# Layer 1 of a four-layer model: its preparation in a written order, the second half's decays among the chunks, the experts six steps later

## The chip, the cores and the metric

The kernel runs on one core of a Trainium2 chip. A core has five engines with queues of their own: TensorE (PE; its weight loads are shown as PEld), VectorE (DVE), ScalarE (ACT), GpSimd (POOL) and SyncE (SP), which here only issues transfers. The metric is device time in microseconds (us) from launch to end; lower is better. Each engine works through its queue in order, and an instruction that waits holds up everything behind it on its engine.

## The reference, cut to what matters

The model has four layers, each an attention-like part plus a feed-forward part on the same normed input. The kernel has B = 2 sequences of S = 1024 tokens with D = 128. The change is in layer 1 alone: gated slot attention (4 heads, K = V = 32, M = 64 slots) beside a mixture of eight experts with the top two picked.

```python
xn = _layernorm(x, axis=-1)
x = x + _L1_attn_ref(xn, ...) + _L1_ffn_ref(xn, ...)

# attention
q = _swish((x @ Wq).reshape(b, t, H, K))
k = _swish((x @ Wk).reshape(b, t, H, K))
v = (x @ Wv).reshape(b, t, H, V)
f = jax.nn.log_sigmoid((x @ Wf).reshape(b, t, H, M)) / GATE_LOGIT_NORMALIZER   # 8
s = 1.0 - jnp.exp(f)
def step(carry, inp):
    hk, hv = carry
    q_t, k_t, v_t, s_t, g_t = inp
    ge = jnp.exp(g_t)
    hk = hk * ge[:, :, None, :] + k_t[..., :, None] * s_t[..., None, :]
    logits = jnp.einsum('bhk,bhkm->bhm', q_t * scale, hk)
    p = jax.nn.softmax(logits, axis=-1)
    hv = hv * ge[..., :, None] + s_t[..., :, None] * v_t[..., None, :]
    return ((hk, hv), jnp.einsum('bhm,bhmv->bhv', p, hv))
o = o * rsqrt(mean(o * o) + NORM_EPS) * g_norm_w
return o.reshape(b, t, H * V) @ Wo

# experts
probs = jax.nn.softmax(x @ gate_w.T, axis=-1)
top2_w, top2_idx = jax.lax.top_k(probs, 2)
h = jax.nn.relu(jnp.einsum('th,ehf->tef', x, W1) + b1)
y = jnp.einsum('teh,ehf->tef', h, W2) + b2
out = jnp.einsum('te,tef->tf', comb, y)
```

## The kernel before

Activations lie transposed in SBUF: `xT` and the normed `xnT` are 128 features by 2048 tokens in f32, batch 0 in the first 1024 columns. `layer1` (L1612) norms, then runs two generators in turn: `l1_gsa`, the attention, and `l1_experts`. Each `yield` is a mark; `in_turn` (L1076) goes from mark to mark of the attention, numbers them n, and after each mark for which `when(n)` holds lets the experts go one piece further.

`l1_gsa` first prepares (up to L1393), with three PSUM buffers of two banks. For each batch: queries and keys (`l_pq`, L1344, Silu on ACT), then keys and values by rows (`l_pk`, L1353: `l_kt` by ACT, `l_vt` by DVE). Then four gate units, each one half of the slots (a) of one batch over all 1024 tokens: `l_pz` is the product with Wf; ACT does Abs, Exp, Ln (L1366 to L1368), DVE the subtraction that makes the log gate (L1369), ACT exponentials of plus and minus an eighth of it (`l_up`, `l_g`), and DVE the decays: 1 - g into `l_sf`, one scan for `l_ef` and one for its inverse `l_r` (L1381, a running product that starts anew every 128 tokens), and three products into `l_sf`. ACT loads a table whenever it changes among Silu, Exp and Ln. `stat` and `c.bad` collect whether the decays stayed in range. In this part a planner set the order of the instructions on each engine.

Then come 16 chunks j (n = j // 2 is the 128 tokens, b = j % 2 the batch), in an order written out by hand (`manual_schedule`, L1523), with four marks to a chunk. For chunk j: `l_pa`, masked into `l_at` (`pairs`); `l_sf` and `l_ef` turned by PE into `l_pr`, copied to `l_se` by ACT (`turned`); the logits `l_lg`, DVE's `l_p` and `l_m`, four Exp on ACT (`logits`); DVE's shares (`shares`); the end decay `l_pd`, `l_dk`; the states `l_pu`, `l_hk`, `l_hv`; and one chunk later the turned shares `l_pp`, `l_pt`, the weights `l_pw`, `l_wt` and the outputs `l_po`, copied into `l_oT`. `l_po` and `l_pu` share one PSUM buffer. After the loop the outputs are normed (`l_ms`) and multiplied with Wo.

The experts' pieces (`moe_sparse`, L746): the routing (`l1_route`: weights `r_w_t`, logits `r_lg`, softmax, both top picks); the rows turned (`m_pr`, `m_rows`) and each token's slot (`places`: `m_used`, `m_rank`, ..., `m_to`, `m_back`); 32 scatters of 128 rows each on POOL's queue into the slots in DRAM (L780), in four pieces; loads of the first two experts by SP; then for each of eight experts four pieces: rows in (`m_pt`, `m_xeT`), first product (`m_ph`, `m_h`), second product (`m_py`, `m_yT`), rows out (`m_pb`, `m_ye`, stored by SP), with the load for the expert after next; then eight pieces that gather two tiles of rows each (four gathers on POOL's queue, L840, one piece ahead), weigh them (`m_rows`) and turn them back (`m_back`) into xT. With `lead=2` two pieces come before the attention's first mark; four follow in the preparation, the experts begin at mark 14 (chunk 2), and from 48 on every second mark has a piece.

Of the kernel before, what the change touches and what calls it, by code (L numbers as in the profile page):

```python
# [10 lines left out]
F32 = mybir.dt.float32  # L11
BF16 = mybir.dt.bfloat16
I32 = mybir.dt.int32
AF = mybir.ActivationFunctionType
# [4 lines left out]
P = 128  # L19
# [1264 lines left out]
def l1_gsa(c, w, xnT, oT):  # L1284
# [7 lines left out]
    with ExitStack() as es:  # L1292
# [34 lines left out]
        stat = wp.tile([P, 4 * NTB], F32, tag="stat", name="stat")  # L1327

        q, k, kt, vt = ([None] * B for _ in range(4))
        ef, sf = [], []  # L1330

        qds = []
        for n in range(4):
            qds.append(wp.tile([P, L1_H, P], F32, tag=f"qd{n}", name=f"l1_qd{n}"))
            nc.gpsimd.memset(qds[n], 0.0)
        with tc.tile_pool(name="g_ps0", bufs=3, space=PSUM) as ps:
            for b in range(B):
                xb = xnT[:, b * S : (b + 1) * S]
                q[b] = sb.tile([P, S], F32, tag=f"q{b}", name=f"l1_q{b}")
                k[b] = sb.tile([P, S], F32, tag=f"k{b}", name=f"l1_k{b}")  # L1340
                for n, dst in enumerate((q[b], k[b])):
                    pq = ps.tile([P, S], F32, tag="mm", name=f"l1_pq{b}_{n}")
                    mm_wide(c, pq, wqk[:, n, :], xb)
                    nc.scalar.activation(dst, pq, AF.Silu)  # L1344
                kt[b] = sb.tile([P, NTB, D], F32, tag=f"kt{b}", name=f"l1_kt{b}")
                vt[b] = sb.tile([P, NTB, D], F32, tag=f"vt{b}", name=f"l1_vt{b}")
                for g in range(2):
                    gs = slice(4 * g, 4 * g + 4)
                    pk = ps.tile([P, 4, 2, D], F32, tag="mm", name=f"l1_pk{b}_{g}")
                    for n in range(4):  # L1350
                        t = 4 * g + n
                        mm(c, pk[:, n], xb[:, t * P : (t + 1) * P], wkv.rearrange("p a d -> p (a d)"))
                    nc.scalar.activation(kt[b][:, gs, :], pk[:, :, 0, :], AF.Silu)  # L1353
                    nc.vector.tensor_copy(vt[b][:, gs, :], pk[:, :, 1, :])
                yield
            for b in range(B):
                xb = xnT[:, b * S : (b + 1) * S]
                ef.append(sb.tile([P, 2, S], F32, tag=f"ef{b}", name=f"l1_ef{b}"))
                sf.append(sb.tile([P, 2, S], F32, tag=f"sf{b}", name=f"l1_sf{b}"))
                for a in range(2):  # L1360
                    pz = ps.tile([P, S], F32, tag="mm", name=f"l1_pz{b}_{a}")
                    mm_wide(c, pz, wf[:, a * P : (a + 1) * P], xb)
                    at = 2 * b + a

                    g = wk.tile([P, S], F32, tag="g", name=f"l1_g{b}_{a}")
                    nc.scalar.activation(g, pz, AF.Abs)  # L1366
                    nc.scalar.activation(g, g, AF.Exp, scale=-1.0)
                    nc.scalar.activation(g, g, AF.Ln, bias=1.0)  # L1368
                    nc.vector.scalar_tensor_tensor(g, pz, 0.0, g, ALU.min, ALU.subtract)  # L1369
                    up = wk.tile([P, S], F32, tag="up", name=f"l1_up{b}_{a}", bufs=1)  # L1370
                    nc.scalar.activation(up, g, AF.Exp, scale=-0.125)
                    nc.scalar.activation(g, g, AF.Exp, scale=0.125)
                    s = sf[b][:, a, :]
                    nc.vector.tensor_scalar(s, g, -1.0, 1.0, ALU.mult, ALU.add)

                    e = ef[b][:, a, :]
                    r = wk.tile([P, S], F32, tag="r", name=f"l1_r{b}_{a}", bufs=1)
                    for x, y in ((g, e), (up, r)):
                        nc.vector.tensor_copy(first[:, 0:S:P], x[:, 0:S:P])
                        nc.vector.memset(x[:, 0:S:P], 0.0)  # L1380
                        nc.vector.tensor_tensor_scan(y, x, first, 0.0, ALU.mult, ALU.add)  # L1381
                    nc.vector.tensor_scalar(
                        stat[:, at * NTB : (at + 1) * NTB], e[:, P - 1 : S : P], 1e-14, None, ALU.is_ge
                    )

                    tt(c, g, e, r, ALU.mult)
                    nc.vector.scalar_tensor_tensor(g, g, 2.0, r, ALU.subtract, ALU.mult)
                    nc.vector.scalar_tensor_tensor(s, g, -1.0, s, ALU.mult, ALU.mult)
                    yield

            ok = wp.tile([P, 1], F32, tag="ok", name="l1_okp")
            nc.vector.tensor_reduce(ok, stat, AX.X, ALU.min)
            nc.vector.tensor_scalar(c.bad[:, 1:2], ok, 0.5, None, ALU.is_lt)  # L1393

        with tc.tile_pool(name="g_ps", bufs=1, space=PSUM) as ps:
            NJ = B * NTB
# [13 lines left out]
            def pairs(j):  # L1410
# [4 lines left out]
                ats[j] = wk.tile([P, L1_H, P], F32, tag="at", name=f"l1_at{tag}")  # L1415
                tt(c, ats[j], pa, bcast_mid(upto, L1_H), ALU.mult)

            def turned(j):

                n, b, ts, tag = where(j)  # L1420
                pr = ps.tile([P, 2, 2 * P], F32, tag="pr", name=f"l1_pr{tag}")
                for a in range(2):
                    nc.tensor.transpose(pr[:, 0, a * P : (a + 1) * P], sf[b][:, a, ts], c.ident)
                for a in range(2):
                    nc.tensor.transpose(pr[:, 1, a * P : (a + 1) * P], ef[b][:, a, ts], c.ident)
                ses[j] = wk.tile([P, 2, 2 * P], F32, tag="se", name=f"l1_se{tag}", bufs=3)
                nc.scalar.copy(ses[j], pr)

# [37 lines left out]
            def weights(j):  # L1466
                n, b, ts, tag = where(j)

                pw = ps.tile([P, 2, 2, 2 * P], F32, tag="pw", name=f"l1_pw{tag}")
                for h in range(L1_H):  # L1470
                    a, r = divmod(h, 2)
                    rows = slice(HF * r, HF * r + HF)
                    mm(c, pw[:, r, a, 0:P], sf[b][rows, a, ts], pts[j][rows, a, :])
                wts[j] = wk.tile([P, 2, 2, P], F32, tag="wt", name=f"l1_wt{tag}")
                tt(c, wts[j].rearrange("p r a t -> p (r a) t"), pw.rearrange("p r a t -> p (r a) t")[:, :, 0:P],
                   bcast_mid(upto, 4), ALU.mult)
# [20 lines left out]
            def states(j, dk):  # L1497

                n, b, ts, tag = where(j)
                ss = ses[j][:, 0, :]  # L1500
                pu = ps.tile([P, HM + P], F32, tag="pu", name=f"l1_pu{tag}")
                mm(c, pu[:, 0:HM], kt[b][:, n, :], ss)
                for a in range(2):
                    mm(c, pu[:, HM + a * HF : HM + (a + 1) * HF], ss[:, a * P : (a + 1) * P],
                       vt[b][:, n, a * HF : (a + 1) * HF])
                nk = wk.tile([P, HM], F32, tag=f"hk{b}", name=f"l1_hk{tag}")
                nv = wk.tile([P, 2, HF], F32, tag=f"hv{b}", name=f"l1_hv{tag}")
                uk, uv = pu[:, 0:HM], pu[:, HM:].rearrange("p (a v) -> p a v", v=HF)
                if n:
                    tt(c, nk, uk, hk[b], ALU.add)  # L1510
                    uk = nk
                    tt(c, nv, uv, hv[b], ALU.add)
                    uv = nv
                tt(c, nk, uk, dk.rearrange("p h m -> p (h m)"), ALU.mult)
                end = (n + 1) * P - 1
                for a in range(2):
                    nc.vector.scalar_tensor_tensor(
                        nv[:, a, :], uv[:, a, :], ef[b][:, a, end : end + 1], vmask.rearrange("p a v -> p (a v)"),
                        ALU.mult, ALU.mult,
                    )  # L1520
                hk[b], hv[b] = nk, nv

            with tc.manual_schedule():  # L1523
# [2 lines left out]
                pairs(0)  # L1526
                turned(0)
                old = {}
                for j in range(NJ + 1):
                    if j:  # L1530
                        turn_shares(j - 1)
                    if j < NJ:
                        old[j] = hv[j % B]
                        logits(j)
                        yield
                    if j:
                        weights(j - 1)
                    if j < NJ:
                        if j + 1 < NJ:
                            pairs(j + 1)  # L1540
                        yield
                        if j + 1 < NJ:
                            turned(j + 1)
                        shares(j)
                        if j < NJ - B:
                            dk = end_decay(j)
                        yield
                    if j:
                        outputs(j - 1, old.pop(j - 1))
                    if j < NJ:  # L1550
                        yield
                        if j < NJ - B:
                            states(j, dk)
# [58 lines left out]
def layer1(c, w, xT, xnT, general=False):  # L1612
    nc, tc = c.nc, c.tc
    layernorm_all(c, xT, xnT, 1e-5, "n1")
    with tc.tile_pool(name="l1", bufs=1) as sb:
# [3 lines left out]
        with tc.tile_pool(name="e1", bufs=1) as s2, tc.tile_pool(name="e1_ps", bufs=2, space=PSUM) as ps:  # L1619
# [4 lines left out]
            else:  # L1624

                in_turn(
                    l1_gsa(c, w, xnT, oT), moe, lead=2,
                    when=lambda n: n < 4 or 14 <= n < 47 or (n > 47 and n % 2 == 0),
                )
        if general:  # L1630
            l1_gsa_scan(c, w, xnT, oT)
# [640 lines left out]
```

## Time and profile before

| | us |
|---|---|
| median of 3 runs | 2033.06 (2029.17 to 2038.33) |
| the profiled execution | 2022.65 |
| its span, first to last instruction | 2020.9 |
| its mean granted TensorE clock | 0.882 |

Busy time by layer, from the profile's stretches (the borders are read from the timeline; a stretch has norm and experts in it):

| stretch, us | what | PE | DVE | ACT | POOL | clock |
|---|---|---|---|---|---|---|
| 0 to 1160 | layer 0 | 1008.5 | 692.7 | 808.0 | 73.7 | 0.92 |
| 1160 to 1425 | layer 1 | 186.2 | 145.6 | 150.1 | 82.2 | 0.77 |
| 1425 to 2021 | layers 2 and 3 | 439.9 | 425.9 | 307.8 | 257.7 | 0.85 |

In layer 1, by line:

| line, engine | what | count | mean ns |
|---|---|---|---|
| L1381 DVE | scans over 128x1024 | 8 | 2290 |
| L1369 DVE | log gate, 128x1024 | 4 | 1216 |
| L63, L1387, L1388 DVE | the three products, 128x1024 each | 12 | 1219 |
| L1366 to L1368, L1371, L1372 ACT | Abs, Exp, Ln, Exp, Exp, 128x1024 | 20 | 1050 |
| ACT | table loads, 1179 to 1265 | 12 | 1283 |
| L780 POOL | scatters | 32 | 1459 |

How it is read: times count from the span's first instruction. A busy PE is not PE at its peak, since matmuls are pipelined and their ends modelled; a clock of 1.00 is full speed, 0.50 half. An f32 product shows as two records for each of its instructions. In the names of the profile, buffer numbers are left out: `l_pz` is every gate product.

### The profile page before, as it was taken

How to read it: one execution, taken by the hardware profiler on the slowest of the kernel's cores; microseconds unless marked ns; L12 is line 12 of the kernel's file. 1: busy time of each engine (PE TensorE's matmuls, PEld its weight loads, DVE VectorE, ACT ScalarE, POOL GpSimd, SP SyncE). 2: the span in 40 equal slices, each digit the busy share in tenths (PEclk: the TensorE clock that was granted, in tenths of full speed). 3: DMA queues.
4: the chain of work that ended last, by engine and by line, in shares of the span. 5: the costliest groups of instructions: out<-in, count | busy, mean ns of one | idle time of the engine just before them, and what ended most of it. 6: DMA issues, size and time to landing. Idle time of an engine off the chain costs nothing. (4 is left out here: it accounts for less than half of the span.)

```text
span 2020.9 us, 18408 instructions
## 1 busy us (share of the span) xinstructions
PE 1634.6 (81%) x5978; PEld 730.2 (36%) x5978; DVE 1264.2 (63%) x2130; ACT 1265.9 (63%) x2116; POOL 413.6 (20%) x413
## 2 busy tenths in 40 slices
PE   4699999999688789988888772987785999566784
PEld 2232322222234334433333340654332444223563
DVE  4788866881365446446556338554457998785673
ACT  3378756786477787887877665654556778223451
POOL 2000000000000200000300017033056666761110
PEclk7799989999788899999999885986787999778897
DMA  4521110100100210100100001110014443100000
GB/s 107 161 63 32 25 26 2 25 1 2 48 6 12 62 31 26 31 21 16 38 5 0 8 12 35 58 43 23 9 37 152 136 161 102 42 15 18 6 6 12
DMA packets 76817, 81.66 MB, mean 40 GB/s; under 512 B 12759, under 2 KB 57590, under 8 KB 75560
## 3 DMA queue, kind: packets, MB, share of 16 engines
q1 hardware_dynamic: 67224, 62.68, 10.5%
q0 software_dynamic: 7888, 16.93, 3.4%
q8 instruction: 49, 0.80, 0.2%
q10 hardware_dynamic: 1600, 0.79, 0.2%
q14 instruction: 56, 0.46, 0.1%
HBM read 55.18 MB, written 24.44 MB: 39 GB/s over the span
## 5 line engine op out<-in xcount | busy, mean ns | idle before, releaser
L487 DVE TENSOR_REDUCE maxes<-sc 128x1 f32<-128x1024 f32 x256 | 303.6, 1219 | 79.1 <-PE sc L51 78.3
L602 ACT ACTIVATE ex<-st 128x512 f32<-128x512 f32 x512 | 277.1, 599 | 102.9 <-PE st L51 97.5
L51 PE MATMUL st<-qst,kst 75*128 75x512 bf16 x512 | 178.7, 391 | 8.4 <-DMA qst<-mt 5.6
L51 PE MATMUL sc<-kst,qst 72*128 72x512 bf16 x512 | 161.1, 399 | 28.0 <-DMA kst<-scr 14.1
L1786 POOL TENSOR_TENSOR su<-dx,bb 128x512 f32<-128x512 f32 x128 | 162.3, 1273 | 83.1 <-DVE sh L1797 76.2
L780 POOL DMA_INDIRECT m_x<-m_rows,m_to x80 | 98.6, 1232 | 335.6 <-DVE m_back L742 188.8
L840 POOL DMA_INDIRECT m_yg<-m_y,m_back x80 | 79.8, 998 | 422.9 <-DVE a_y L1045 311.2
L51 PE MATMUL py<-spr,ident 128*128 128x512 f32 x256 | 146.9, 658 | 0.0
L1792 ACT ACTIVATE da<-dt,am 128x512 f32<-128x512 f32 x128 | 87.6, 690 | 83.4 <-DVE sh L1797 79.4
L51 PE MATMUL av<-ex,va 128*9 128x512 f32 x1024 | 139.2, 613 | 0.0
L51 PE MATMUL a_ph<-a_x,wf 128*128 128x512 f32 x256 | 122.6, 614 | 12.7 <-DVE a_x L1046 9.3
L51 PE MATMUL a_pf<-a_h,wf 128*128 128x512 f32 x256 | 114.1, 599 | 0.0
L51 PE MATMUL pc<-cst,sel 80*128 80x512 bf16 x128 | 52.8, 413 | 74.9 <-DVE spr L63 71.0
L51 PEld LDWEIGHTS <-kst 75*128 75x128 bf16 x512 | 49.1, 98 | 168.9 <-issue 126.3
L1007 ACT ACTIVATE a_h<-a_ph,cols 128x512 f32<-128x512 f32 x128 | 84.9, 687 | 33.4 <-PE a_ph L51 33.2
L51 PEld LDWEIGHTS py<-spr,ident 128*128 128x128 f32 x256 | 53.3, 209 | 126.4 <-issue 99.9
L51 PE MATMUL a_pQ<-a_y,wqkvo 128*128 128x512 f32 x56 | 48.0, 1007 | 53.7 <-DVE a_y L1046 53.7
L63 DVE TENSOR_TENSOR spr<-sh,pc 128x512 f32<-128x512 f32 x128 | 85.3, 667 | 8.1 <-PE pc L51 7.9
L63 DVE TENSOR_TENSOR a_r<-a_r,a_x 128x512 f32<-128x512 f32 x32 | 22.0, 690 | 99.1 <-ACT a_r L1018 99.1
L1797 DVE TENSOR_TENSOR_SCAN sh<-da,su 128x512 f32<-128x512 f32 x64 | 77.9, 1217 | 7.5 <-POOL su L1786 4.0
L51 PEld LDWEIGHTS <-qst 72*128 72x128 bf16 x512 | 51.5, 101 | 85.7 <-issue 45.4
L1797 DVE TENSOR_TENSOR_SCAN sh<-da,carry,su 128x512 f32<-128x512 f32 x64 | 81.7, 1276 | 0.2 <-ACT carry L1839 0.2
(541 smaller groups left out, 3224.0 us busy)
## 6 DMA issues: line engine op xcount, KB each, us to landing
bb<-bd SPq DMA_DIRECT2D x64, 256.0 KB
m_w<-in_L_ffn_w_dram SPq DMA_DIRECT2D x44, 128.0 KB
m_xe<-m_x SPq DMA_DIRECT2D x22, 256.0 KB
m_y<-m_ye SPq DMA_DIRECT2D x22, 256.0 KB
qst<-scr POOLq DMA_DIRECT2D x24, 192.0 KB, 9.1
kst<-scr SPq DMA_DIRECT2D x24, 192.0 KB
wf<-in_L_attn_Wf_dram SPq DMA_DIRECT2D x16, 256.0 KB
m_x<-zero SPq DMA_DIRECT2D x1, 3584.0 KB
```

The lines of the kernel that those rows point to most:

```text
L51: c.nc.tensor.matmul(out, lhsT, rhs, start=start, stop=stop)
L63: c.nc.vector.tensor_tensor(out, a, b, op)
L487: nc.vector.tensor_reduce(mx[:, t % HT, i : i + 1], sc, AX.X, ALU.max)
L602: nc.scalar.activation(ex, st, AF.Exp)
L780: nc.gpsimd.indirect_dma_start(views[K * t + k][:, :], bass.IndirectOffsetOnAxis(ap=to[:, k, t : t + 1], axis=0), rows[:, t, :], None)
L840: nc.gpsimd.indirect_dma_start(g, None, ys[:, :], bass.IndirectOffsetOnAxis(ap=back[:, k, t : t + 1], axis=0))
L1007: nc.scalar.activation(half(b, f"h{f}", o, "h", f"h{l}_{b}_{f}_{o}", bufs=8), ph, AF.Gelu_apprx_tanh, bias=c.cols["bf1"][:, 4 * l + f : 4 ...
L1786: nc.gpsimd.tensor_tensor(us[k], dx[b, a][:, o * CH : (o + 1) * CH], bb[2 * b + o, s], ALU.mult)
L1792: nc.scalar.activation(das[k], dt[b, a][:, o * CH : (o + 1) * CH], AF.Exp, scale=am[:, a, s : s + 1])
L1797: nc.vector.tensor_tensor_scan(hs[k], das[k], us[k], carry[b, a][:, s : s + 1] if o else 0.0, ALU.mult, ALU.add)
```

## The change

The order of the preparation is written out, under `manual_schedule`, and its marks change. A gate unit is now one half of the tokens (u) of one batch with both halves of the slots, so `ef` and `sf` have four tiles of 128x2x512 in place of two of 128x2x1024; the scans run over 512 columns; Abs and Exp write into `ef` itself, and `r` lies in `up`. The first halves of both batches come first (products, logs, exponentials), then a mark with the routing behind it, then the second halves' products and logs and the first unit's decays, then five marks (slots, scatters). Queries, keys and values follow, with the second unit's decays around them. The second halves' exponentials and decays are done one piece at a time among the chunks (`more()`, one at each mark; two units, eight pieces each: chunks 0 to 3). `lead=2` goes; the experts' pieces come at marks 0 to 5, 20 to 58 and then at every even one, where the preparation has six marks as before: experts begin at the last mark of chunk 3 in place of chunk 2's.

```diff
+        UNITS = [(b, u) for u in range(2) for b in range(B)]
...
+        def gate_products(b, u, ps):
+            pz = pzs[b, u] = ps.tile([P, 2, CH], F32, tag="mm", name=f"l1_pz{b}_{u}")
+            for a in range(2):
+                mm(c, pz[:, a, :], wf[:, a * P : (a + 1) * P], xnT[:, b * S + u * CH : b * S + (u + 1) * CH])
+
+            f = ef[b, u]
+            nc.scalar.activation(f, pz, AF.Abs)
+            nc.scalar.activation(f, f, AF.Exp, scale=-1.0)
+
+        def gate_logs(b, u):
+            nc.scalar.activation(ef[b, u], ef[b, u], AF.Ln, bias=1.0)
+
+        def log_gates(b, u):
+            nc.vector.scalar_tensor_tensor(ef[b, u], pzs[b, u], 0.0, ef[b, u], ALU.min, ALU.subtract)
+
+        def gate_exps(b, u):
+            up = ups[b, u] = wk.tile([P, 2 * CH], F32, tag="up", name=f"l1_up{b}_{u}")
+            nc.scalar.activation(up, flat(ef[b, u]), AF.Exp, scale=-0.125)
+            g = gs[b, u] = wk.tile([P, 2 * CH], F32, tag="g", name=f"l1_g{b}_{u}")
+            nc.scalar.activation(g, flat(ef[b, u]), AF.Exp, scale=0.125)
+
+        def gate_decays(b, u):
+            g, up, e, s = gs[b, u], ups[b, u], flat(ef[b, u]), flat(sf[b, u])
+            nc.vector.tensor_scalar(s, g, -1.0, 1.0, ALU.mult, ALU.add)
+            yield
+            r = up
+            for x, y in ((g, e), (up, r)):
+                nc.vector.tensor_copy(first[:, 0:S:P], x[:, 0:S:P])
+                nc.vector.memset(x[:, 0:S:P], 0.0)
+                for a in range(2):
+                    cs = slice(a * CH, (a + 1) * CH)
+                    nc.vector.tensor_tensor_scan(y[:, cs], x[:, cs], first[:, cs], 0.0, ALU.mult, ALU.add)
+                    yield
...
+            tt(c, g, e, r, ALU.mult)
+            yield
+            nc.vector.scalar_tensor_tensor(g, g, 2.0, r, ALU.subtract, ALU.mult)
+            yield
+            nc.vector.scalar_tensor_tensor(s, g, -1.0, s, ALU.mult, ALU.mult)
+            yield
+
+        def later_gates():
+            for b, u in UNITS[B:]:
+                gate_exps(b, u)
+                yield from gate_decays(b, u)
...
+        with tc.tile_pool(name="g_ps0", bufs=3, space=PSUM) as ps, tc.manual_schedule():
+            early, late = UNITS[:B], UNITS[B:]
+            for un in early:
+                gate_products(*un, ps)
+            for un in early:
+                gate_logs(*un)
+                log_gates(*un)
+            for un in early:
+                gate_exps(*un)
+            yield
+            for un in late:
+                gate_products(*un, ps)
+            for un in late:
+                gate_logs(*un)
+            for _ in gate_decays(*early[0]):
+                pass
+            for un in late:
+                log_gates(*un)
+            for _ in range(5):
+                yield
...
+            decays = gate_decays(*early[1])
+            next(decays)
+            queries_keys(0)
+            for _ in range(4):
+                next(decays)
+            queries_keys(1)
+            for _ in decays:
+                pass
...
+                rest = later_gates()
+
+                def more():
+                    next(rest, None)
...
                     if j < NJ:
                         old[j] = hv[j % B]
                         logits(j)
+                        more()
                         yield
...
                 in_turn(
-                    l1_gsa(c, w, xnT, oT), moe, lead=2,
-                    when=lambda n: n < 4 or 14 <= n < 47 or (n > 47 and n % 2 == 0),
+                    l1_gsa(c, w, xnT, oT), moe,
+                    when=lambda n: n < 6 or 20 <= n < 59 or (n > 59 and n % 2 == 0),
                 )
```

`queries_keys(b)` holds the old loop body for one batch. `more()` stands ahead of each of the four marks of a chunk, and the chunks read their half through `gate_half`. In a step with an expert the built order on PE changes from `l_lg, m_pb, l_pw, l_pa, m_pt, l_pr, l_pd, m_ph, l_po, m_py, l_pu, l_pp` to `l_lg, m_ph, l_pw, l_pa, m_py, l_pr, l_pd, m_pb, l_po, m_pt, l_pu, l_pp`; on ACT from `Exp x4, m_ye, m_xeT, l_se, m_h, l_oT, m_yT, l_qd x4, l_pt` to `Exp x4, m_h, m_yT, l_se, m_ye, l_oT, m_xeT, l_qd x4, l_pt`. On ACT the table loads of the preparation are, in order, Ln, Exp, Ln, Silu and Exp. The queues of POOL and SP keep their order. Outside layer 1 nothing moves.

More of the change, by code (lines that the diff above doesn't have):

```diff
@@ L1329, in l1_gsa @@
         q, k, kt, vt = ([None] * B for _ in range(4))
-        ef, sf = [], []
         qds = []
@@ L1335, in l1_gsa, with flat @@
             nc.gpsimd.memset(qds[n], 0.0)
-        with tc.tile_pool(name="g_ps0", bufs=3, space=PSUM) as ps:
-            for b in range(B):
+        ef, sf = {}, {}
+        UNITS = [(b, u) for u in range(2) for b in range(B)]
+        for b, u in UNITS:
+            ef[b, u] = sb.tile([P, 2, CH], F32, tag=f"ef{b}_{u}", name=f"l1_ef{b}_{u}")
+            sf[b, u] = sb.tile([P, 2, CH], F32, tag=f"sf{b}_{u}", name=f"l1_sf{b}_{u}")
+        pzs, gs, ups = {}, {}, {}
+        def flat(t):
+            return t.rearrange("p a s -> p (a s)")
@@ new lines, in log_gates @@
+        def log_gates(b, u):
[17 more added lines that the diff above has]
+                    yield
+            at = UNITS.index((b, u))
+            nc.vector.tensor_scalar(stat[:, at * NTB : (at + 1) * NTB], e[:, P - 1 : S : P], 1e-14, None, ALU.is_ge)
+            tt(c, g, e, r, ALU.mult)
[4 more added lines that the diff above has]
+            yield
@@ new lines, in later_gates, with queries_keys @@
+        def later_gates():
+            for b, u in UNITS[B:]:
+                gate_exps(b, u)
+                yield from gate_decays(b, u)
+            ok = wp.tile([P, 1], F32, tag="ok", name="l1_okp")
+            nc.vector.tensor_reduce(ok, stat, AX.X, ALU.min)
+            nc.vector.tensor_scalar(c.bad[:, 1:2], ok, 0.5, None, ALU.is_lt)
+        with tc.tile_pool(name="g_ps0", bufs=3, space=PSUM) as ps, tc.manual_schedule():
[18 more added lines that the diff above has]
+                yield
+            def queries_keys(b):
@@ L1347, in l1_gsa @@
                 for g in range(2):
-                    gs = slice(4 * g, 4 * g + 4)
+                    sl = slice(4 * g, 4 * g + 4)
                     pk = ps.tile([P, 4, 2, D], F32, tag="mm", name=f"l1_pk{b}_{g}")
@@ L1352, in l1_gsa @@
                         mm(c, pk[:, n], xb[:, t * P : (t + 1) * P], wkv.rearrange("p a d -> p (a d)"))
[L1353 to L1389, printed above, removed]
@@ L1391, in l1_gsa @@
-            ok = wp.tile([P, 1], F32, tag="ok", name="l1_okp")
-            nc.vector.tensor_reduce(ok, stat, AX.X, ALU.min)
-            nc.vector.tensor_scalar(c.bad[:, 1:2], ok, 0.5, None, ALU.is_lt)
+                    nc.scalar.activation(kt[b][:, sl, :], pk[:, :, 0, :], AF.Silu)
+                    nc.vector.tensor_copy(vt[b][:, sl, :], pk[:, :, 1, :])
+            decays = gate_decays(*early[1])
[3 more added lines that the diff above has]
+                next(decays)
@@ L1416, in pairs, with gate_half @@
                 tt(c, ats[j], pa, bcast_mid(upto, L1_H), ALU.mult)
+            def gate_half(n, b, gates):
+                o = n * P % CH
+                return gates[b, n * P // CH], slice(o, o + P)
             def turned(j):
                 n, b, ts, tag = where(j)
+                s, es = gate_half(n, b, sf)
+                e, es = gate_half(n, b, ef)
                 pr = ps.tile([P, 2, 2 * P], F32, tag="pr", name=f"l1_pr{tag}")
                 for a in range(2):
-                    nc.tensor.transpose(pr[:, 0, a * P : (a + 1) * P], sf[b][:, a, ts], c.ident)
+                    nc.tensor.transpose(pr[:, 0, a * P : (a + 1) * P], s[:, a, es], c.ident)
                 for a in range(2):
-                    nc.tensor.transpose(pr[:, 1, a * P : (a + 1) * P], ef[b][:, a, ts], c.ident)
+                    nc.tensor.transpose(pr[:, 1, a * P : (a + 1) * P], e[:, a, es], c.ident)
                 ses[j] = wk.tile([P, 2, 2 * P], F32, tag="se", name=f"l1_se{tag}", bufs=3)
@@ L1469, in weights @@
                 pw = ps.tile([P, 2, 2, 2 * P], F32, tag="pw", name=f"l1_pw{tag}")
+                s, es = gate_half(n, b, sf)
                 for h in range(L1_H):
@@ L1472, in weights @@
                     rows = slice(HF * r, HF * r + HF)
-                    mm(c, pw[:, r, a, 0:P], sf[b][rows, a, ts], pts[j][rows, a, :])
+                    mm(c, pw[:, r, a, 0:P], s[rows, a, es], pts[j][rows, a, :])
                 wts[j] = wk.tile([P, 2, 2, P], F32, tag="wt", name=f"l1_wt{tag}")
@@ L1514, in states @@
                 tt(c, nk, uk, dk.rearrange("p h m -> p (h m)"), ALU.mult)
-                end = (n + 1) * P - 1
+                e, es = gate_half(n, b, ef)
+                end = es.stop - 1
                 for a in range(2):
                     nc.vector.scalar_tensor_tensor(
-                        nv[:, a, :], uv[:, a, :], ef[b][:, a, end : end + 1], vmask.rearrange("p a v -> p (a v)"),
+                        nv[:, a, :], uv[:, a, :], e[:, a, end : end + 1], vmask.rearrange("p a v -> p (a v)"),
                         ALU.mult, ALU.mult,
@@ L1540, in l1_gsa @@
                             pairs(j + 1)
+                        more()
                         yield
@@ L1546, in l1_gsa @@
                             dk = end_decay(j)
+                        more()
                         yield
@@ L1550, in l1_gsa @@
                     if j < NJ:
+                        more()
                         yield
```

## The prediction

> **What bounds the kernel now.** I read the page's chain of waits first: it goes through every layer, so only the path inside layer 1 can move the end. The busy times by stage cut layer 1 into its parts (columns: stretch, length, then busy time and count of PE, PEld, DVE, ACT, POOL, then the granted clock):
>
> ```profile
> 1205.00:1248.00 43.00, 7.88 (x14) 2.70 (x13) 29.48 (x36) 30.41 (x28) 35.08 (x27) 0.58 0.12 38
> 1248.00:1275.00 27.00, 17.71 (x89) 12.58 (x90) 21.34 (x41) 9.69 (x32) 10.77 (x6) 0.65 0.16 49
> 1275.00:1340.00 65.00, 64.09 (x445) 44.04 (x444) 39.06 (x105) 43.93 (x152) 0.00 (x0) 1.00 0.16 48
> 1340.00:1408.00 68.00, 48.91 (x272) 33.25 (x270) 31.48 (x84) 25.46 (x100) 30.89 (x32) 0.71 0.12 34
> ```
>
> From 1205 to 1248 PE does almost nothing: the gates run on ACT and DVE, and POOL scatters the tokens meanwhile. From 1275 to 1340 PE is full at clock 1.00: eight experts, one to a chunk. The last stretch is the gathers with the last chunks. The timelines (start, duration, engine, line, operation) give the marks:
>
> ```profile
> 1179.74 3.78 PE L51 MATMUL l_pq<-xnT,l_wqk 128*128 128x512 f32 x4 [4.83 <-DVE xnT L63]
> ...
> 1248.02 2.04 PE L51 MATMUL l_pa<-l_qd,l_k 128*128 128x512 f32 x2 [30.55 <-DVE l_g L1369]
> ...
> 1275.54 0.49 PE L804 MATMUL m_pt<-ident,m_xe 128*128 128x128 f32 x3
> ```
> ```profile
> 1204.16 1.01 POOL L780 DMA_INDIRECT m_x<-m_rows,m_to  x1 [61.42 <-DVE l_vt L1354]
> ...
> 1222.44 2.18 POOL L780 DMA_INDIRECT m_x<-m_rows,m_to  x1 [0.30 <-issue]
> ...
> 1257.39 2.90 POOL L780 DMA_INDIRECT m_x<-m_rows,m_to  x1 [0.30 <-issue]
> ...
> 1344.32 0.99 POOL L840 DMA_INDIRECT m_yg<-m_y,m_back  x1 [84.03 <-DVE l_hk L63]
> ```
>
> So: chunks start at 1248.0, the first expert at 1275.5, its slots filled by 1260.3 and loaded soon after. The gathers start at 1344.3, 5.8 after the last expert's transposes (1338.5), and the norm's products follow at 1408.25, 63.9 after the gathers start. One expert step, 8.13 from one logits product to the next (1304.71 to 1312.84):
>
> ```profile
> 1304.71 0.60 PE L51 MATMUL l_lg<-l_hk,l_q 128*128 128x256 f32 x2
> ...
> 1309.46 0.91 PE L51 MATMUL m_ph<-m_xeT,m_w 128*128 128x384 f32 x2
> 1310.30 0.44 PE L51 MATMUL l_po<-l_pt,l_hv 128*64 128x128 f32 x4
> 1310.67 0.43 PE L51 MATMUL l_po<-l_wt,l_vt 128*32 128x128 f32 x8
> 1311.05 0.91 PE L51 MATMUL m_py<-m_h,m_w 128*128 128x384 f32 x2
> ```
>
> Between m_ph and m_py, PE has l_po to do while ACT turns m_ph into m_h (1310.41, 0.58); m_py starts when both end.
>
> **The change part by part.** All times are on the clock of the profiled execution. Both versions begin at 1179.74, released by the last xnT.
>
> *Gates first.* ACT: l_pz of batch 0 ends near 1183.5 (the 3.78 row, half clock), then two Abs and two Exp of about 1.07, a table load of 1.28, two Ln: 1191.2. DVE subtracts twice (1.22) to 1192.6. Only then does DVE copy r_w_t, which before ran at 1183.76; queued behind that wait stand r_lg on PE and the routing on DVE. r_lg takes 4.0 in its row; after 7 idle I take 5.7: to 1198.5. Seven of twelve table loads go (9.0 of ACT); that is worth nothing here because DVE ends last. Softmax and both top picks, 6 to 1204.45.
>
> *Unit 0's decays before the slots.* DVE then does one half sequence: 9.6, from the unit's 9.5 in the old timeline (1220.60 to 1230.70 less a foreign 0.6) with each 2.29 scan cut in two of 1.2 (a 128x512 scan in layer 2 has 1.22 to 1.28). Two late subtractions 2.4, then m_used and m_rank: 1217.7. The slot arithmetic takes 3.7 without the copies between; scatters start at 1222.3 instead of 1204.2, **18 later**. Thirty-two at a pitch of 1.28 are 41; each long scan held POOL up by some 1.9 (2.18 and 2.37 rows above against 0.97), so eight to ten half scans add 8 to 10: done near 1273. SP issued the load 1.5 after the last scatter (1261.77), and its traffic ended about 2.7 later: m_xe near 1277. SP's order is unchanged, so the loads queued behind it move along.
>
> *Queries and keys.* PE holds them behind m_rank (1217.5): 16 products and 16 half ones, 14.7 at full clock plus 2 for a cold start, to 1233.3; l_pa waits for the last l_vt copy: **1234.7, 13.3 earlier** than 1248.0. The first logits, after l_at: 1237.1 against 1252.8.
>
> *Late decays among chunks 0 to 3.* A chunk alone needs 5.3 of DVE (the sum of one step's rows). ACT's two late Exp (2.15) stand behind the chunk's four Exp, and DVE's first late instruction waits for them in order, 3.6 each in chunks 0 and 2; behind it wait l_at, l_wt and so l_pa, l_po on PE. DVE's queue from the first l_p (1238.1) to the second: 2.0 (l_p, l_m, the rest of unit 1's last product), the wait 3.6, then 7.6 (l_sf 0.6, l_at 0.6, three half scans with their copies 4.3, shares and l_dk 1.3, states 0.8): 13.2. The next chunk has no wait: 9.1. Chunks 2 and 3 add up to 13.4 and 9.7, as their states have two adds more. The fifth l_p comes at 1238.1 + 45.4 = 1283.5. An l_p follows its logits by 1.55, so the fifth step stands as if its logits were at 1281.95; before, they were at 1288.46: **6.5 ahead**. m_pt stands after the third l_po, 1277.3, just when m_xe lands, and has 3 of slack.
>
> *Experts six marks later.* At the fifth chunk the old kernel has done its second expert's first part; now it begins the first one's products. And the order in a step changes: m_ph comes after the logits, m_py two products later, m_h behind the four Exp. From logits at 0: l_p 1.55, l_m, the four Exp 2.53 to 3.87, m_h to 4.45, m_py at 4.51. PE would be there at 1.27 + 0.84 + 0.65 + 0.96 = 3.72. It **waits 0.8**; after that m_py .75, l_pr .44, l_pd .53, m_pb .42, l_po .74, m_pt .33, and l_pu waits 0.1 for l_oT: l_pu .82, l_pp .22: next logits at **8.86 instead of 8.13**. Seven steps: 1281.95 + 62.0 = 1344.0; the last m_pb at +6.2, 1350.2. m_ye now follows m_pb directly, not behind four Exp, so the gathers start 3.9 after it (0.1 + 0.5 + 0.5 copy, 2.8 store as before): **1354.1, 9.8 later**.
>
> *The tail.* Before, each of four groups of eight gathers was followed by a whole chunk: four returns 13.0 to 13.6 apart, the first 12.4 after the gathers start. Now the second return follows the first with no logits between, so it is bound by POOL alone, 8 x 1.26 = 10.1; the third then 11, as l_po stands ahead; the fourth 13. Sum 47 and 11.9 to l_ms: 58.9, **5.0 less**.
>
> Sum: 9.8 - 5.0 = **+4.8**. The profiled 2022.65 would become 2027.5. That execution lies 10.4 under the median of 2033.06 and under the lowest run, so I put the difference on the median: **2038**.
>
> Not in the trace: whether PE's clock holds. After 4.83 idle it was granted 0.50 (1179 to 1183), after 0.4 it stayed at 1.00 (1269 to 1273), after waits of 2.4 it fell to 0.70 (1349 to 1357). 0.8 is nearest the second: full clock in the steps. Bounds: 0 from that row; at the other end the half-clock step, where a logits row takes 1.49 for 1.00, half as much again on 8 of PE work, so 4 a step.
>
> The Trainium skill, in "TensorE: Matmul & The Clock Gate", section "What's actually happening", has half rate after an idle window of about 3.4 us. That speaks against the seven idle us ahead of r_lg and agrees with 0.50 after 4.83, while 0.70 after 2.4 is lower than it says. By the rule alone the expert steps stay warm and the estimate is the same +4.8.
>
> **Rivals.** *A, the lead gets through (faster).* Chunks are 15.7 ahead at the first logits. If ACT's m_h comes in time (8.13 a step), 5.1 goes; if the tail is the gathers alone (40.3 + 2.2 + 11.9 = 54.4), another 4.5. For it: PE has the same instructions. Against: the four Exp and m_h are on one queue. Together -4.8: 2028. Faster by over 0.5% (10.2) would need the routing not to wait for the gates as well.
>
> *B, the cold clock (slower).* PE is mostly idle through chunks 0 to 3, so it enters the experts at half clock; with a stall in each step it may not recover. For it: the old tail, with stalls of 2 to 3 a chunk, ran at 0.58. Against: 0.8 is short. Two cold steps cost 8 (2046), all eight 32 (2070). It passes the 0.5% bound from the second cold step.
>
> *C, the scatters decide.* If each of the 32 took the old mean pitch of 1.75 (56.1 in all), they end at 1278.4, m_xe lands at 1282.6, 5.3 late, 3 of it slack: +2.3, 2040. Against: fewer scans fall in. A scatter start later than reckoned passes on whole.
>
> **How the numbers follow.** Forecast: 0.40; A as priced: 0.10; C as priced: 0.08; these three lie within 0.5% (about what a measurement of this kernel can tell from no change), 0.58 together. B, or a scatter start so late that it does the same: 0.34. A with the routing early too: 0.08. Low end: A's 2028 less 2 for the median's own scatter (2029 to 2038); high end: B with two to three cold steps and C, 2052. The likeliest case alone spans 2032 to 2044.
>
> **What would show it.** In the new profile: scatters from about 1222; l_pa near 1235; first m_pt near 1277; logits 8.9 apart with m_py released by ACT's m_h; gathers from about 1354; clock 1.0 in the expert stretch. Wrong if the step stays at 8.13 (then -5), if the clock there is below 0.9 (then B), or if the scatters start before 1215 (then everything after the routing is earlier).

## The result, and the profile after

The changed kernel is slower: median 2051.58 us of 8 runs (2034.69 to 2055.26) against 2033.14 of 8 runs of the kernel before beside it (2029.17 to 2039.89), ratio 1.0073 [1.0053, 1.0093]. Two later jobs, each with the kernel before beside it, gave 1.0065 [1.0041, 1.0089] and 1.0100 [1.0074, 1.0126]. The profiled execution took 2055.26, with a span of 2053.5.

The same four stretches as in the prediction (stretch, length, busy time and count of PE, PEld, DVE, ACT, POOL, granted clock, share and rate of the transfers), now of the changed kernel:

```profile
1205.00:1248.00 43.00, 25.24 (x98) 16.67 (x97) 34.18 (x66) 24.24 (x43) 19.48 (x18) 0.85 0.08 25
1248.00:1275.00 27.00, 14.83 (x68) 10.70 (x68) 13.89 (x28) 7.90 (x27) 15.80 (x15) 0.67 0.23 70
1275.00:1340.00 65.00, 58.26 (x367) 39.45 (x367) 42.90 (x107) 34.79 (x122) 0.00 (x0) 0.89 0.14 41
1340.00:1408.00 68.00, 39.74 (x241) 25.64 (x239) 27.64 (x73) 25.41 (x89) 29.80 (x32) 0.78 0.12 38
```

The first stretch is what the change is about: PE works 25 us in it where it had 8, while POOL's share falls from 35 to 19, since the scatters now start late. The second is the surprise: PE, DVE and ACT are all less busy than before (14.8, 13.9 and 7.9 against 17.7, 21.3 and 9.7), in the middle of the chunks. Nobody works, so something is waited for.

The marks on the timeline of the changed kernel, in the order of the prediction's (gates, first scatter, first chunk, last scatter, first expert, first gather, norm products):

```profile
1178.76 3.78 PE L51 MATMUL l_pz<-xnT,l_wf 128*128 128x512 f32 x4 [4.83 <-DVE xnT L63]
1223.34 1.05 POOL L780 DMA_INDIRECT m_x<-m_rows,m_to  x1 [81.59 <-DVE m_kept L768]
1235.25 1.10 PE L51 MATMUL l_pa<-l_qd,l_k 128*128 128x512 f32 x2 [1.50 <-DVE stat L1382]
1267.11 0.96 POOL L780 DMA_INDIRECT m_x<-m_rows,m_to  x1 [0.31 <-issue]
1287.29 0.55 PE L804 MATMUL m_pt<-ident,m_xe 128*128 128x128 f32 x3
1364.48 0.99 POOL L840 DMA_INDIRECT m_yg<-m_y,m_back  x1 [96.41 <-DVE l_hv L63]
1434.52 2.08 PE L51 MATMUL l_ms<-l_sq,hmean 128*128 128x512 f32 x2 [0.38 <-ACT l_oT L1549]
```

This execution starts layer 1 one us earlier than the profiled one of before (1178.76 against 1179.74). The first scatter and the first chunk stand within 2 us of the forecast; the first expert is 10 late, the gathers 10, the norm products 22. What stands between is in the waits, the number in brackets, of the chunks and of the gathers:

```profile
1259.88 0.58 ACT L1488 COPY l_se<-l_pr 128x512 f32<-128x512 f32 x1 [6.07 <-remote]
1264.85 0.27 ACT L1549 COPY l_oT<-l_po 128x128 f32<-128x128 f32 x1 [4.38 <-remote]
1265.16 1.22 PE L51 MATMUL l_pu<-l_se,l_kt 128*128 128x256 f32 x2 [9.53 <-ACT l_oT L1549]
1268.40 0.42 DVE L63 TENSOR_TENSOR l_hk<-l_pu,l_dk 128x256 f32<-128x256 f32 x1 [5.00 <-PE l_pp L1523]
...
1390.02 0.27 ACT L1549 COPY l_oT<-l_po 128x128 f32<-128x128 f32 x1 [9.54 <-remote]
1390.85 0.95 POOL L840 DMA_INDIRECT m_yg<-m_y,m_back  x1 [4.01 <-ACT m_rows L857]
```

How this is read: l_se copies what PE's l_pr wrote. PE's record has l_pr ending at 1254.20, yet ACT starts at 1259.88, and the profile, finding no instruction that ended then, calls the releaser "remote". On one core nothing is remote: the ends of PE's records are modelled, and the product came later than its record. Every reader of PE says so: l_wt, l_at, l_se, l_dk and l_oT start at 1253.49, 1255.62, 1259.88, 1260.59 and 1264.85, while the records of what they read end at 1251.34, 1253.35, 1254.20, 1255.05 and 1255.64. The trace also has the moments at which PE raised the semaphore that they wait for: 1253.47, 1255.60, 1259.85, 1260.57 and 1264.82, each within 0.03 of the reader's start. So the work that PE's records place between 1250.1 and 1255.6 was done at 1264.8. At 1379 to 1390 it happens again, and there even POOL's gathers stop, because ACT, stuck before l_oT, can't free their buffers. I call this a slow stretch.

### The profile page after: what moved, and what is told of

Read it like the earlier page. It is cut to its first block, busy times and chain, and to the rows that moved or that the text cites. A ratio compares the mean times of both kernels' runs of the same rounds, so it can differ in the third digit from the quotient of the medians.

```text
span 2053.5 us, 18407 instructions
## 1 busy us (share of the span) xinstructions
PE 1650.7 (80%) x5978; PEld 739.2 (36%) x5978; DVE 1266.9 (62%) x2138; ACT 1257.6 (61%) x2109; POOL 400.7 (20%) x413
## 3 DMA queue, kind: packets, MB, share of 16 engines
q1 hardware_dynamic: 67224, 62.68, 10.4%
## 5 line engine op out<-in xcount | busy, mean ns | idle before, releaser
L780 POOL DMA_INDIRECT m_x<-m_rows,m_to x80 | 86.5, 1081 | 355.9 <-DVE m_back L742 188.9
L51 PE MATMUL a_ph<-a_x,wf 128*128 128x512 f32 x256 | 122.6, 614 | 12.7 <-DVE a_x L1046 9.3
L51 PEld LDWEIGHTS py<-spr,ident 128*128 128x128 f32 x256 | 53.6, 210 | 126.2 <-issue 99.7
L63 DVE TENSOR_TENSOR spr<-sh,pc 128x512 f32<-128x512 f32 x128 | 85.6, 669 | 10.8 <-PE pc L51 10.6
```

The lines of the kernel that those rows point to most:

```text
L51: c.nc.tensor.matmul(out, lhsT, rhs, start=start, stop=stop)
L63: c.nc.vector.tensor_tensor(out, a, b, op)
L780: nc.gpsimd.indirect_dma_start(views[K * t + k][:, :], bass.IndirectOffsetOnAxis(ap=to[:, k, t : t + 1], axis=0), rows[:, t, :], None)
```

## The experiments

All jobs ran the kernel before beside the kernels tried; times compare within a job only, because each job had a machine of its own: the kernel before took 2033.13 in the first (again, phase, warm, nolate), 2022.41 in the second (control, noscat, both), 2027.07 in the third (again2, control2, first) and 2025.35 in the fourth (warm2, noscat2).

**Is it a pause that only some executions have?** `again` is the changed kernel once more.

> The changed kernel once more, unaltered. Theory P (the excess over the forecast is a pause of TensorE that only some executions have): the times fall again into two groups, near 2037 and near 2053, with nothing between 2042 and 2048; where the profiled execution is of the short group, ACT's l_se and l_oT copies (L1488, L1549) do not stand still for 6.07 and 4.38 us, l_p of the third chunk comes near 1260 to 1263 and the first gather near 1354. Theory C (the planned course itself is 15 us longer than forecast, by the half clock that the record shows in 1245-1255, 1259-1269 and 1276-1286): one group near 2052 and the same waits in every profile.

2046.06 (2039.15 to 2056.59), 1.0065. Theory P fell: the times spread over 17 us without two groups. Of C the waits held, not the single group: the profiled execution has the same course as the first, the l_p's 12.8, 18.5, 12.9 and 9.3 apart, with nearly the same waits (l_se 5.33, l_oT 4.40). Every profile of the changed kernel, `again2` below too, has the slow stretch in the chunks. But no profile shows one of its short executions (down to 2034.69 in the first eight), so whether those have it is open.

**The two parts of the change that the forecast had priced.** `phase` moves the experts' marks by two, `nolate` writes the late decays into the preparation:

```diff
-    when=lambda n: n < 6 or 20 <= n < 59 or (n > 59 and n % 2 == 0),
+    when=lambda n: n < 6 or 18 <= n < 57 or (n > 57 and n % 2 == 0),
```
```diff
             queries_keys(1)
             for _ in decays:
                 pass
+            for _ in later_gates():
+                pass
...
-                rest = later_gates()
-
                 def more():
-                    next(rest, None)
+                    pass
```

> Only the experts' marks are moved, two earlier (loads at mark 18, transposes of an expert's rows again right behind a chunk's l_pa, as in the kernel before). If m_py waits for m_h behind the four Exp, a step falls from 8.87 to 8.13-8.2 us, 8 steps save 5.5, and the two marks save up to 4 more where m_xe is there: 2029-2033 for the short group, 15 more for the long one. Rival: if the step is long for another reason (the clock, PE's own work), it stays at 8.8-8.9 and only the 0 to 4 us of the earlier start come off: 2034-2038 and 2049-2053.

2045.88 (2040.86 to 2048.64), 1.0061 [1.0046, 1.0075]: no gain. Yet the step did what was expected. One step of `after` and one of `phase` on PE's timeline:

```profile
1310.11 0.60 PE L51 MATMUL l_lg<-l_hk,l_q 128*128 128x256 f32 x2
1311.38 0.86 PE L51 MATMUL m_ph<-m_xeT,m_w 128*128 128x384 f32 x2
...
1314.59 0.91 PE L51 MATMUL m_py<-m_h,m_w 128*128 128x384 f32 x2 [0.64 <-ACT m_h L813]
...
1318.98 0.60 PE L51 MATMUL l_lg<-l_hk,l_q 128*128 128x256 f32 x2
```
```profile
1301.68 0.91 PE L51 MATMUL m_ph<-m_xeT,m_w 128*128 128x384 f32 x2 [0.45 <-ACT m_xeT L806]
1303.27 0.91 PE L51 MATMUL m_py<-m_h,m_w 128*128 128x384 f32 x2
```

In the first, 8.87 from logits to logits and m_py waits for m_h; in the second m_py waits for nothing, and the l_p's stand 8.13 apart. The gathers start 176.7 us after layer 1 does (185.7 in `again`), 9 earlier; but from the gathers to the norm products it takes 72.9 in place of 66.3, and the first product to the norm products 249.6 in place of 252.0. So 6.6 of the 9 were lost again at the gathers, where the slow stretches are. Not all of that need be theirs: `both` below, with the same marks and `nolate`'s decays, takes 61.0 there on a machine without slow stretches, where `noscat` takes 56.5.

> The late half's decays stand at the end of the preparation again instead of among the chunks. By the forecast's terms: l_pa about 2 x 9.6 us later (near 1254), and the four gaps of 13.2, 9.1, 13.4 and 9.7 us between the l_p's shrink to 5.5-7, so the fifth chunk comes 0 to 4 us earlier: 2034-2039. Theory F: PE is idle in one piece before 1254 and busy from then on, so one group of times. Theory S: the scatters end at 1268 and overlap with two chunks only, so the pause is shorter but not gone. If the decays among the chunks cost nothing, the time is 15 to 19 us longer.

2040.33 (2028.9 to 2042.84), 1.0025 [1.0011, 1.0038], the fastest changed kernel of this job. The expectation was wrong about the order: l_pa came at 1235.5, not 1254, because the late decays still ran among the chunks: DVE works on them from 1239.6 to 1262.9, mixed with the chunks' own instructions from the first to the third l_p. The l_p's were 14.3, 12.0, 7.6 and 6.3 apart: 40.2 in all, where `again` has 53.5.

These chunks have no slow stretch, although the machine is that of `again` and the scatters run beside them until 1269 (ACT's timeline of `nolate`, then POOL's last scatter):

```profile
1256.87 0.56 ACT L1490 COPY l_se<-l_pr 128x512 f32<-128x512 f32 x1
1257.34 0.26 ACT L1551 COPY l_oT<-l_po 128x128 f32<-128x128 f32 x1
```
```profile
1269.11 0.97 POOL L780 DMA_INDIRECT m_x<-m_rows,m_to  x1 [0.30 <-issue]
```

PE raised its semaphore for l_pr at 1254.80 and for l_po at 1256.63, where their records end (1254.78 and 1256.59). `both`, on the machine without slow stretches, has the same first two gaps: 14.36 and 12.05, against 14.35 and 12.04 here. So scatters beside the chunks are not enough to make a slow stretch. What in this order keeps it away was not tried.

**What the machine has to do with it.** `control` and `control2` are the kernel before, `again2` the changed one, `noscat` the changed one without the 32 scatters of layer 1:

```diff
     for t in range(NT):
-        for k in range(K):
+        for k in range(0 if name == "m1" else K):
             nc.gpsimd.indirect_dma_start(
```

> The kernel before, unaltered, profiled once more: its first profile (2022.65 us) lies 10 us under the median of its runs (2033). Theory P (slow stretches of TensorE between 1250 and 1390 belong to the changed order): the new profile shows none of them, the l_p's of layer 1 stand 13.2, 5.9, 7.8 and 8.1 us apart as in the first, and 10 us are missing elsewhere. Theory E (every execution may have them, and the first profile of before happened to have none): l_po or m_back near the first gathers ends 3 to 10 us behind its record, as at 1380-1390 in the changed kernel, and the span is near 2031.

2020.54, in a job in which the kernel before takes 2022.41. No slow stretch, every interval in layer 1 like that of the first profile. Theory E was not refuted by this: the next job settled it.

> The changed kernel without the 32 scatters of layer 1's rows (the experts get rows of zeros). Theory S (TensorE is slowed by the scatters that run beside chunks 0 to 3): l_se and l_oT of the second and third chunk come without the waits of 6.07 and 4.38 us, the gap between l_p 2 and l_p 3 falls from 18.5 to 9-10 us, and the time falls by 8-10 us. Theory F (TensorE runs slowly after a gap, whatever else runs): the gap stays at 17-19 us, and the time falls by 0-3 us.

2021.23 (2019.99 to 2027.83), 0.9998 [0.9985, 1.0011]. The gap was 8.8, but on a machine without any slow stretch, so the theories weren't told apart here. What the run does show is the planned course undisturbed (the table below).

> The changed kernel once more. The kernel before took 2033 us in the jobs in which the changed one took 2046 to 2052, and 2022 in the job of the control. Theory M (the machine decides: where the kernel before takes 2022, TensorE shows no slow stretches in either kernel): 4 to 6 us over the kernel before of this job, and a course like that of the run without scatters (l_p's 12.7, 8.8, 12.9, 9.3 apart, gathers from 1354 to 1356, norm products at 1411 to 1413); where it takes 2033, 12 to 19 over it, with l_se and l_oT standing still for 4 to 6 us. Rival S (the scatters slow TensorE everywhere): 18.5 between the second and the third l_p on this job too, whatever the kernel before takes.

2047.83 (2043.01 to 2053.55), 1.0100 [1.0074, 1.0126], on a machine where before takes 2027.07: 20.8 over it, a little more than theory M's 19. l_se and l_oT waited 3.06 and 5.73, and the second and the third l_p were 18.8 apart.

> The kernel before, profiled on the same chip as the changed one. Where its runs take 2033: slow stretches of TensorE in it too, 10 to 12 us in all, most of them not in chunks 0 to 3 (its l_p's stay 13.3, 5.9, 7.8, 8.1 apart) but at the gathers or after layer 1. Where its runs take 2022: none.

2031.95. The kernel before has slow stretches there too: in layer 1 none in chunks 0 to 3 (13.3, 5.9, 7.8, 8.1), all at the gathers. The same copies in `control2` and in `control`:

```profile
1358.79 0.27 ACT L1487 COPY l_oT<-l_po 128x128 f32<-128x128 f32 x1 [5.08 <-remote]
1365.81 0.42 DVE L63 TENSOR_TENSOR l_hk<-l_pu,l_hk 128x256 f32<-128x256 f32 x1 [9.51 <-remote]
```
```profile
1357.71 0.27 ACT L1487 COPY l_oT<-l_po 128x128 f32<-128x128 f32 x1 [3.07 <-PE l_po L51]
1360.03 0.42 DVE L63 TENSOR_TENSOR l_hk<-l_pu,l_hk 128x256 f32<-128x256 f32 x1 [2.88 <-PE l_pu L51]
```

Counted from the layer's start, l_hk comes 6.7 us later than on the other machine, with the same program. So the first profile of before, 10 under its median, was one without slow stretches.

**What slows TensorE.** `warm` and `warm2` put idle products into PE's gaps to hold its clock up; `noscat2` is `noscat` again.

```diff
                        vt[b][:, n, a * HF : (a + 1) * HF])
+                if j < 4:
+                    for _ in range(26):
+                        mm(c, pu[:, HM + P :], c.ident, c.ident)
```

(`pu` is 128 columns wider for it. `warm` has 16 for j < 5; `warm2` also 13 ahead of l_po.)

> 16 products of the identity with itself stand in TensorE's queue behind l_pu of chunks 0 to 4, into columns that nothing reads: 16 x 0.14 to 0.27 us of work in gaps of 4 to 6 us. Theory F (the pauses belong to a clock that goes up and down because PE has gaps between chunks 0 and 5): the clock stays up from 1237 to 1300, there is one group of times, at 2034-2040. Rival S (the pauses come from the scatters that run at the same time, or from elsewhere): two groups 15 us apart as before, the short one at 2037-2042.

2065.57 (2059.74 to 2072.39), 1.0164 [1.0143, 1.0185]: worse, with 26.4 between the second and the third l_p. The clock still fell, at 1249.8, so the theory wasn't tested yet.

> As warm, with enough idle products (26 behind l_pu and 13 ahead of l_po in chunks 0 to 3, some 0.12 us each at full clock, in columns that nothing reads) to fill PE's gaps until the experts begin. In warm the granted clock still fell, at 1249.8, after a gap of 2.04 us, and the slow stretch followed. Theory F (a slow stretch follows a fall of the clock from 1.0 to 0.5 while work stands in the queue, on machines where the kernel before takes 2027 or more): the clock stays at 1.00 from 1222 to 1300, no wait of 4 us for PE in chunks 0 to 3, l_p's 13 to 15, 9 to 11, 13 to 15 and 9 to 11 apart, first m_pt by 1284. Rival W (the more PE works, the more it is slowed): as in warm, a gap of 20 us or more between two l_p's although the clock on record stays up, 2065 or more. Where the kernel before takes 2022 in this job, neither is told apart.

2064.61 (2062.32 to 2069.51), 1.0194 [1.0169, 1.0218]. A stretch of the busy times, then PE's and ACT's timelines:

```profile
1240.00:1250.00 10.00, 7.68 (x68) 7.51 (x66) 6.51 (x13) 3.94 (x11) 7.87 (x8) 1.00 0.17 52
```
```profile
1246.43 0.38 PE L1523 MATMUL l_pp<-ident,l_p 128*128 128x128 f32 x2
1256.57 1.22 PE L51 MATMUL l_pw<-l_pt,l_sf 64*128 64x128 f32 x8 [8.89 <-issue]
```
```profile
1256.15 0.37 ACT L1525 COPY l_pt<-l_pp 128x256 f32<-128x256 f32 x1 [12.17 <-remote]
```

The clock was granted in full until 1250.7, and l_pp, recorded to 1246.81, reached ACT at 1256.15. The full clock lasted 3.9 us beyond the end of that record, so the delay began before the clock fell: theory F falls. W, that more work makes it slower, fits both runs (24.0 and 20.0 between the first l_p's), but nothing tested it alone.

> The changed kernel without the scatters again, since the kernel before took 2022 us in the job of its first run, and there neither kernel showed a slow stretch. On a machine where the kernel before takes 2027 or more: theory S (the slow stretch needs the scatters beside it): gap between the second and the third l_p 9 us, as in the first run. Theory F (it needs only the fall of the clock, here at 1246): 14 to 19 us, although nothing is scattered. Where the kernel before takes 2022 in this job: 8.8 again, and the question stays open.

2035.89 (2032.46 to 2037.93), 1.0049 [1.0030, 1.0068], in the same job and on the same machine as `warm2`, with a slow stretch at the gathers as usual (l_oT at 1377.86 after 8.60 "remote"). In the chunks, ACT's copies in `noscat2`:

```profile
1252.91 0.59 ACT L1488 COPY l_se<-l_pr 128x512 f32<-128x512 f32 x1 [0.43 <-PE l_pr L1486]
1254.38 0.27 ACT L1549 COPY l_oT<-l_po 128x128 f32<-128x128 f32 x1 [0.88 <-PE l_po L51]
```

No slow stretch: 12.7, 8.7, 12.9 and 9.3 between the l_p's. And the clock moved as in the changed kernel, here by the busy times of `noscat2`:

```profile
1248.00:1275.00 27.00, 21.68 (x105) 15.11 (x104) 22.91 (x50) 10.85 (x41) 0.00 (x0) 0.69 0.00 1
```

0.69 against 0.67 above, and DVE works 22.9 in place of 13.9. So the chunks' slow stretch needs the scatters, though by `nolate` it needs something more as well. This rests on one profile, and the changed kernel did not run in this job. As a whole `noscat2` is 10.5 over the kernel before of its job, where the changed kernel was 12.9 to 20.8 over in its three jobs. The stretches that are left lie beside POOL's gathers, the other indirect transfers; no run left those out.

**A better version.** `both` joins `phase` and `nolate`; `first` is `both` with the routing first and the experts a chunk earlier (`lead=2`, marks 0 to 3, 14 to 52, then every even one).

> The late half's decays in the preparation, and the experts two marks earlier, together. If the two effects add: the steps fall from 8.87 to 8.15 us (8 steps, 5.5 us less than 2040.3), and the two marks save up to 4 where m_xe is there: 2031-2035. Rival: as with the marks alone (2045.9 against 2046.1), what the steps gain is lost in the stretch of the gathers: 2038-2041.

2021.26 (2017.76 to 2025.72), 0.9996 [0.9985, 1.0007], on the machine without slow stretches. The steps stand 8.13 apart and layer 1 is 2.3 us shorter than in `control`; in the whole time that can't be measured.

> As the run with both edits (late decays written into the preparation, experts' marks in their old place in the chunk), and the routing and the slots come first again, so that the experts begin a whole chunk earlier. If the scatters start near 1205 again and end near 1255, m_xe is there by 1262, the first m_pt comes near 1268 instead of 1277, the gathers near 1338 instead of 1346 and the time is 6 to 9 us less than that of both, 0.996 to 0.997 of the kernel before. Rival: the routing delays the gates by its own time (6 to 9 us of DVE ahead of the decays), l_pa comes that much later, and nothing is gained: 0.999 to 1.001.

2028.15 (2025.77 to 2032.51), 1.0006 [0.9991, 1.0022]. The scatters start at 1209.6 and the gathers 155.7 after the layer's start, 8.9 earlier than in `control2`, but then 79.3 pass to the norm products in place of 70.9. The rival in the expectation has the number, not the reason: l_pa came 51.8 after the layer's start, earlier than the 56.5 of `both`. No version beat the kernel before.

## Why the prediction was wrong, though its range held

It said 2038 and no change to be measured (0.58), slower with 0.34; measured were 2051.58 and slower, just inside its upper bound of 2052. That it lies inside is luck: the upper end was made of two to three cold expert steps (rival B) and late scatters (rival C), and neither came. Layer 1 in intervals, each a difference of two starts (layer 1's first product, first l_p, fifth l_p, first gather, norm products):

| us | to first l_p | to fifth l_p | to first gather | to norm products | sum |
|---|---|---|---|---|---|
| before, first profile | 75.2 | 35.1 | 54.3 | 63.9 | 228.5 |
| control | 75.2 | 35.1 | 54.3 | 63.9 | 228.5 |
| control2 | 75.2 | 35.1 | 54.3 | 70.9 | 235.5 |
| forecast of the change | 58.4 | 45.4 | 70.6 | 58.9 | 233.3 |
| noscat (machine of control) | 59.9 | 43.7 | 72.2 | 56.5 | 232.3 |
| noscat2 (a machine with slow stretches) | 59.9 | 43.7 | 72.2 | 66.5 | 242.3 |
| again2 (machine of control2) | 59.9 | 53.8 | 72.2 | 66.7 | 252.6 |
| after | 59.9 | 53.6 | 72.2 | 70.0 | 255.8 |

*Gates first: right.* r_w_t was copied 13.1 after the layer's start (forecast 12.9). r_lg took 6.99 where I took 5.7. The scatters began 20.2 later than before, counted from that start (forecast 18.1), but were done at 1268 where I had 1273: the half scans held POOL up by less than I took.

*Queries and keys, late decays: right within 2 us.* l_pa came 11.8 earlier than before by the same count (forecast 13.3). The four gaps of 13.2, 9.1, 13.4 and 9.7 were 12.7, 8.8, 12.9 and 9.3 where nothing disturbed them. That DVE's queue paces these chunks was so.

*The step: right.* 8.87 for 8.86, with the wait of m_py for m_h, and with the clock at 1.00 through waits of 0.64. The first expert step was 10.6, which makes the 1.6 missing in the third column.

*Where it failed: the sum took the scatters for hidden.* The part on unit 0's decays moved them 18 us later and asked only when their data would be there; the part on queries and keys moved the chunks 13 us earlier. Neither asked what they now lie beside: before, 9 us of chunks (1248 to 1257) had scatters next to them, afterwards 32 (1235 to 1267). From the first to the fifth l_p the stretch costs 53.8 - 43.7 = 10.1 (`again2` against `noscat2`, two machines with slow stretches). It is a term that I left out, not one of a wrong size. The overlap alone does not price it: in `nolate` it is as long (1235 to 1269) and costs nothing.

*The tail: right within 2.4 us where nothing is slow.* 56.5 (forecast 58.9), and 66.3 (`again`) to 70.0 otherwise. Its four terms, 12.4, 10.1, 11 and 13, make 46.5, where I wrote 47. Here the base misled too: I took the 10.4 between the first profile and the median for a constant to be put on top. `control` and `control2` are 11.4 apart, and 7.0 of that lie between the gathers and the norm products, in the very stage that I was pricing.

For `again2` against `control2`, 17.2 in layer 1: plan 232.3 - 228.5 = 3.8, scatters beside the chunks 10.1, gathers (66.7 - 56.5) - (70.9 - 63.9), about 3.3. The first is the forecast's 4.8. As a whole these two executions are 15.2 apart, and the medians of the job 20.8. That the changed kernel takes 3.8 more on the machine of `control` is taken from `noscat`, which has no scatters; itself it never ran there.

*Rival B* has the right size (2046 to 2070) and the wrong cause. By the sign I had named for it, a clock below 0.9 in the expert stretch, it seems confirmed: 0.89 from 1275 to 1340. But that stretch now begins 12 us ahead of the first expert (1287.29). In the expert steps themselves the clock was full, here by the busy times of `after`:

```profile
1300.00:1360.00 60.00, 55.08 (x371) 36.37 (x371) 34.01 (x90) 37.58 (x130) 0.00 (x0) 1.00 0.16 48
```

And from 1248 to 1275 the clock was as low without the scatters, and nothing was lost. A went the wrong way, C's scatters ended at 1268 instead of 1278.

## What to carry to other kernels

When a change moves a block of transfers and another engine's work against each other, write down what each lies beside afterwards; being off the chain of waits doesn't make a transfer harmless, and lying beside it doesn't make it harmful: a run without the transfers, and one with another order, tell. Where readers of TensorE start long after its records end and the releaser is "remote", trust the readers. And profile the kernel before more than once: a profile far from its median has something missing, and it may be missing in the stage in question.

## What was not expected of the hardware

Beside indirect transfers of layer 1 TensorE did, on three of the four machines of these jobs, far less than its records say, at full granted clock too (l_pp of `warm2`). In the first slow stretch it raised its semaphore in steps of 2.13, 4.25, 0.72 and 4.25 us, within 0.02 of whole multiples of 0.71.

Not every such transfer does it. The 9 us of overlap in the kernel before cost nothing, in the changed kernel PE worked from 1223 to 1248 beside the scatters at its usual pace, and `nolate`'s chunks lost nothing beside all of theirs. Layer 0's transfers, with PE busy 14 of 23 us beside the scatters and 22 of 23 beside the gathers, cost nothing either: from its first scatter to layer 1's first product it is 525.8 us in `control2` and 525.7 in `control`. What in the transfers does it, their descriptors, their writes or their completions, was not tried.

One thing is left open that bears on all of it: the ten profiles with slow stretches have 20 to 31 fewer semaphore events of TensorE than its 2188 records that give one, the four without (before, control, noscat, both) lack none. It is not TensorE's events alone: of the events of transfers that land, `control` has 9053 and `control2`, the same program, 7961; `after` has 7610. So it may be the machine, or how the trace is taken on it. Every execution on record lists a span and a granted clock, as a trace gives them; none shows the time without a trace.
